# Turning x for the projections: TensorE transposes replaced by a copy within DRAM and VectorE block transposes, in a two-layer graph network whose order is written out by a planner

## The chip, the cores and the metric

The kernel runs on one core of a Trainium2 chip. The core has five engines that run their own instruction streams side by side: TensorE (PE in the profile; its weight loads are shown apart as PEld), VectorE (DVE), ScalarE (ACT), GpSimd (POOL) and SyncE (SP), which here only issues transfers. Each engine executes its instructions strictly in the order in which the program lists them, and an instruction that waits for a semaphore holds up everything behind it on that engine. Transfers run on 16 DMA engines. The metric is the time of one execution on the device in microseconds (us), and lower is better.

## The reference, cut to what matters

There are 16 graphs (batches) of 1024 nodes with 256 features, and a 0/1 adjacency matrix of 1024 x 1024 for each. Layer 0 is attention with 8 heads of 32 features, masked by the adjacency, then two layer norms and a matrix product; layer 1 is two graph attentions and a feed-forward network.

```python
# layer 0, per graph
q, k, v = heads(x @ Wq), heads(x @ Wk), heads(x @ Wv)
e = q @ k.T;  e = where(e >= 0, e, 0.2 * e)
h = softmax(where(adj > 0, e, NEG), axis=-1) @ v
x1 = layernorm(concat([layernorm(h), x]) @ Wffn.T) + x
# layer 1, per graph
h = gat(gat(x1, adj, W1, a1), adj, W2, a2)       # scores from two vectors, softmax over axis 1
r = layernorm(x1 + h)
out = layernorm(r + relu(r @ w_ff1 + b_ff1) @ w_ff2 + b_ff2)
```

All of it is float32. The products over features need x with its features on the partitions, that is, transposed: xT holds feature c*128 + p on partition p, for c = 0 and 1, and the nodes along the free axis. The change is in how xT is made from x, which lies in DRAM with a node per row.

## The kernel before, in words

The work is cut into 16 batches, one per graph. Within a batch the kernel makes xT in four pairs of node tiles (256 nodes each, `x_pair`), projects q and k (`qk_part`) and v (`v_part`), writes q and k to DRAM as a high and a low half and loads them back stacked for each head (`load_stacks`: the tiles qs and ks), and then goes through 8 heads of 8 key tiles: scores on PE (L615), leaky ReLU on ACT and DVE (L631, L633), the exponential on ACT (L636), the mask by a multiplication on POOL (L640), and the product with v on PE (L655). What follows the heads of a batch is `rest`: the norms, two graph attentions (L877 and L880 on DVE, L915 and L940 on PE) and the feed-forward network (L980 and L1008). The rest of one batch runs beside the heads of the next, and the projections for the batch after are made in the same time, so that in the middle of the run all three are in flight.

The order in which each engine gets its instructions is not written by hand. While the program is being built, a planner (`Order`) simulates the engines with costs given in the code. Every piece of work is a Python generator which yields what it needs next: `on(DVE=365)` for an engine and its planned cost in ns, `take` and `give` for buffers, `wait` and `fire` for events, `pause`, and `load` for transfers on SP (planned as 500 ns of SP each and 3500 ns of latency, or later where the planner's clock for all transfers says so). Among the pieces that could start within 300 ns of the earliest, the planner takes the one with the smallest aim, an absolute due time. The aims come from two tables in units of a slot, which is the planned time of one batch: `AIM` for most of the run and `EARLY` for what belongs to the first two batches. The planner's clock only fixes the order; on the chip, semaphores decide when an instruction runs.

The parts that the change and the steps of the prediction touch are these. `x_pair` (L461) takes a 2 KB buffer of the pool "pair" (18 of them, shared with the adjacency tiles, the q and k halves and others), issues one load of 256 nodes from ACT's queue (L466; 2 KB per partition), takes one of three PSUM banks ("misc"), transposes four 128 x 128 blocks on PE (L372 in `transposes`), copies the bank to xT by DVE or ACT, whichever the planner finds free first (L328 or L330 in `copy`), and fires the event that `qk_part` and `v_part` wait for. The node of row 2p+i of the pair goes to column i*128 + p. xT has two buffers, so that the pairs of the next batch can be made while the present one still uses its own. SP's queue carries the weights, the first batch's adjacency (L424), the halves of q and k (L504), the stacks (L581), x1 stored and fetched (L754, L761) and the output (L1023); ACT's queue carries x (L466) and the adjacency of the other batches (L420).

## Time and profile before

The kernel before takes 4320.45 us, the median of 3 runs (4317.54 to 4321.28). The profile is of one execution.

| what | value |
|---|---|
| time of the profiled execution | 4317.81 us |
| its span, from first to last instruction | 4315.9 us |
| PE busy | 4189.7 us (97%) |
| DVE busy | 3544.8 us (82%) |
| ACT busy | 2942.7 us (68%) |
| POOL busy | 2571.6 us (60%) |
| DMA engines busy, mean of 16 | some 28% |
| mean granted TensorE clock | 0.990 |

Busy time is the time in which an engine had at least one instruction under way. The end of a matmul is modelled, and matmuls overlap each other, so a PE that is busy is not PE at its peak; and the mean duration in a row of PE is that of one instruction from its start to its end, several of which are under way at once. A group of instructions is shown as line, engine, operation, tiles and shapes, then the count, busy time and mean duration, and after the bar the idle time of the engine ahead of them with what ended it.

### The profile page before, as it was taken

Reading aid. Unit: us, or ns where it says so; the run is one execution under the profiler, and the core shown is the slowest. Engines: PE = TensorE matmul, PEld = TensorE weight load, DVE = VectorE, ACT = ScalarE, POOL = GpSimd, SP = SyncE. Lnnn points to the kernel's source line nnn. Section 1 sums busy time; section 2 is a strip of 40 time slices with the busy share of each in tenths; the row PEclk is TensorE's granted clock in tenths of the full one; section 3 lists DMA queues with packets and bytes.
Section 4 is the critical chain, followed back from the end, with each engine's and each line's share of the span. In section 5 each row is a group of like instructions: output and inputs, shape, how many; then the busy total and the mean of one; then the engine's idle time right before and its main releaser. Section 6 shows DMA issues by size and latency. Waiting matters only on the chain.

```text
span 4315.9 us, 76274 instructions
## 1 busy us (share of the span) xinstructions
PE 4189.7 (97%) x30027; PEld 3030.3 (70%) x30027; DVE 3544.8 (82%) x5491; ACT 2942.7 (68%) x4362; POOL 2571.6 (60%) x1161
## 2 busy tenths in 40 slices
PE   8788999999999999999999999999999999999999
PEld 4466677677777777777777777777777777777687
DVE  6878878888888887879879788887889879788853
ACT  6756677777767677776776767677776776767632
POOL 5846467664757656574664757646575674747700
PEclk9999999999999999999999999999999999999999
DMA  6413223322232322323232222322323222222100
GB/s 188 125 54 99 69 76 87 91 72 86 74 94 67 96 84 68 90 71 89 84 84 81 79 81 79 91 73 81 91 74 89 81 84 84 74 79 57 30 20 21
DMA packets 156282, 344.79 MB, mean 80 GB/s; under 512 B 21750, under 2 KB 24332, under 8 KB 155916
## 3 DMA queue, kind: packets, MB, share of 16 engines
q1 hardware_dynamic: 112140, 260.13, 21.0%
q10 hardware_dynamic: 43776, 79.71, 6.6%
q8 instruction: 239, 3.92, 0.4%
q14 instruction: 127, 1.04, 0.1%
HBM read 239.09 MB, written 100.66 MB: 79 GB/s over the span
## 4 chain that ended last, share of the span: by engine, by line
PE 82%; DVE 11%; ACT 3%; POOL 1%; DMA 1%; issue 1%; SPq 0%; ACTq 0%; POOLq 0%; DVEq 0%
PE ps_a L655 17%; PE ps_s L615 11%; PE ps_m L915 10%; PE ps_m L980 9%; PE ps_m L940 9%; PE ps_m L1008 7%; PE ps_m L492 4%; DVE p L633 3%; PE ps_m L792 3%; PE ps_m L824 3%; PE ps_m L795 3%; PE ps_m L524 2%; PE ps_m L372 2%; DVE p L699 2%; POOL p L640 1%; DVE att L880 1%
## 5 line engine op out<-in xcount | busy, mean ns | idle before, releaser
L640 POOL TENSOR_TENSOR p<-p,mask 128x1024 f32<-128x1024 f32 x1024 | 2471.1, 2431 | 1425.5 <-ACT p L636 1044.1
L633 DVE TENSOR_TENSOR p<-p,ps_s 128x1024 f32<-128x1024 f32 x1024 | 1211.3, 1213 | 251.2 <-ACT p L631 248.1
L636 ACT ACTIVATE p<-p 128x1024 f32<-128x1024 f32 x1024 | 1082.2, 1059 | 302.3 <-DVE p L633 276.7
L631 ACT ACTIVATE p<-ps_s 128x1024 f32<-128x1024 f32 x1006 | 986.3, 1021 | 345.2 <-PE ps_s L615 283.0
L615 PE MATMUL ps_s<-qs,ks 128*128 128x512 f32 x2048 | 658.7, 437 | 30.6 <-DVE p L633 27.0
L655 PE MATMUL ps_a<-p,v 128*32 128x256 f32 x8192 | 561.9, 388 | 24.4 <-POOL p L640 24.3
L615 PEld LDWEIGHTS ps_s<-qs,ks 128*128 128x128 f32 x2048 | 352.6, 190 | 266.1 <-issue 114.8
L940 PE MATMUL ps_m<-y,att 128*128 128x256 f32 x2048 | 481.1, 382 | 12.6 <-ACT y L885 11.1
L915 PE MATMUL ps_m<-y,att 128*128 128x258 f32 x2048 | 477.1, 383 | 14.4 <-ACT y L885 12.9
L980 PE MATMUL ps_m<-rT,wf 128*128 128x256 f32 x2048 | 474.3, 383 | 9.4 <-ACT hid L989 4.3
L1008 PE MATMUL ps_m<-wf,hid 128*128 128x256 f32 x2048 | 475.7, 381 | 0.6 <-DVE hid L986 0.6
L915 PEld LDWEIGHTS ps_m<-y,att 128*128 128x128 f32 x2048 | 385.5, 190 | 89.3 <-ACT y L885 13.8
L980 PEld LDWEIGHTS ps_m<-rT,wf 128*128 128x128 f32 x2048 | 381.0, 190 | 85.9 <-issue 14.3
L699 DVE TENSOR_TENSOR p<-p 128x1024 f32<-128x1024 f32 x256 | 410.5, 1604 | 23.6 <-PE ps_a L655 23.4
L940 PEld LDWEIGHTS ps_m<-y,att 128*128 128x128 f32 x2048 | 378.4, 190 | 71.1 <-ACT y L885 11.3
L1008 PEld LDWEIGHTS ps_m<-wf,hid 128*128 128x128 f32 x2048 | 379.1, 190 | 63.6 <-issue 8.2
L655 PEld LDWEIGHTS ps_a<-p,v 128*32 128x32 f32 x8192 | 209.5, 109 | 289.3 <-issue 130.8
L655 PE MATMUL ps_a<-p,minus_ones 128*32 128x256 f32 x6144 | 405.8, 382 | 1.2 <-DVE p L699 1.2
L877 DVE SCALAR_TENSOR_TENSOR att<-first,second 128x1024 f32<-128x1024 f32 x256 | 359.7, 1405 | 32.4 <-ACT first L864 28.3
L880 DVE SCALAR_TENSOR_TENSOR att<-mask,att 128x1024 f32<-128x1024 fp8e4 x256 | 339.5, 1326 | 5.6
L655 PEld LDWEIGHTS ps_a<-p,minus_ones 128*32 128x32 f32 x6144 | 199.1, 111 | 138.3 <-issue 7.9
L885 ACT ACTIVATE y<-y,check 128x258 f32<-128x258 f32 x256 | 131.1, 512 | 220.4 <-DVE check L883 217.9
(101 smaller groups left out, 4330.0 us busy)
## 6 DMA issues: line engine op xcount, KB each, us to landing
qs<-qk_halves SPq DMA_DIRECT2D x256, 256.0 KB, 4.0
ks<-qk_halves SPq DMA_DIRECT2D x256, 256.0 KB, 5.2
adj_i<-in_adj_dram ACTq DMA_DIRECT2D x240, 256.0 KB, 3.1
qk_halves<-high SPq DMA_DIRECT2D x128, 256.0 KB, 2.8
qk_halves<-low SPq DMA_DIRECT2D x128, 256.0 KB, 3.6
xr<-in_x_dram ACTq DMA_DIRECT2D x64, 256.0 KB, 4.7
x_kept<-x SPq DMA_DIRECT2D x64, 256.0 KB, 2.0
x<-x_kept SPq DMA_DIRECT2D x64, 256.0 KB, 5.1
```

The costliest lines, as they stand in the source:

```text
L615: nc.tensor.matmul(ps[:, cols], kk[:, t * P:(t + 1) * P], q[:, cols], start=True, stop=True)
L631: nc.scalar.activation(p, ps, AF.Copy, scale=ALPHA)
L633: nc.vector.tensor_tensor(p, p, ps, op=OP.max)
L636: nc.scalar.activation(p, p, AF.Exp)
L640: nc.gpsimd.tensor_tensor(p, p, mask_of(b, t), op=OP.mult)
L655: nc.tensor.matmul(acc[i * DH:(i + 1) * DH, at:at + QN].rearrange("d (t r) -> d t r", r=DH), w, p.rearrange("k (t i r) -> k i t r", i=4, r ...
L699: nc.vector.tensor_tensor(ps[to], ps[to], ps[by], op=OP.add)
L880: nc.vector.scalar_tensor_tensor(e, mask_of(b, j), -1.0, e, op0=OP.mult, op1=OP.mult, accum_out=sums[:, j:j + 1])
L915: nc.tensor.matmul(pa[:, cols:cols + width], big[:, j, i * P:(i + 1) * P], rows[:, j, :width], start=(j == 0), stop=(j == NT - 1))
L940: nc.tensor.matmul(pa[:, i * D:(i + 1) * D], big[:, j, t * P:(t + 1) * P], y2[:, j, :D], start=(j == 0), stop=False)
L980: nc.tensor.matmul(pa[:, i * 2 * P:(i + 1) * 2 * P], wf1[:, dc, hc * P:(hc + 1) * P], rT[:, dc, :], start=(dc == 0), stop=(dc == DC - 1))
L1008: nc.tensor.matmul(pa[:, i * D:(i + 1) * D], hid[hc // 2][:, hc % 2, i * P:(i + 1) * P], wf2[:, hc, :], start=(hc == 0), stop=False)
```

## The change

x is first copied within DRAM, on SP's queue, so that the 256 features of each node are regrouped: for each of four ranges c, the features c*32 to c*32+31 of both halves (e = 0, 1) of the feature axis are laid side by side for all 256 nodes of the pair. That takes four transfers whose source is in runs of 32 floats (128 bytes). Four more transfers, also on SP's queue, load the result so that range c lies on the partitions 32c to 32c+31; each partition receives 512 bytes in each transfer, from two consecutive nodes. Two block transposes on DVE (`nc.vector.transpose`, which turns each block of 32 x 32 by itself) then write xT directly, one for each half of the features. The load on ACT's queue, the four transposes on PE, the PSUM bank and the copy out of it are gone. The two tables of aims and the length of a slot (253,000 to 251,000 ns) are replaced; names and formulas that use them are the same.

```diff
-    SLOT = 253e3
+    SLOT = 251e3
...
-    AIM = dict(mask0=0.602, x=1.454, x_step=-0.0104, mask=0.9396, mask_step=-0.0101, qk0=0.4907, qk1=1.7441,
...
-               ff_step=0.0063, fast0=0.2312, fast1=0.6979, fast15=1.0127, lead=14.8372)
...
+    AIM = dict(mask0=0.6069, x=0.5014, x_step=0.0732, mask=0.8735, mask_step=-0.1284, qk0=0.5927, qk1=2.165,
...
+               ff_step=-0.3151, fast0=0.0511, fast1=0.8537, fast15=0.9217, lead=25.7163)
...
-    EARLY = dict(x=2.6481, x_step=-0.1001, mask=0.5019, mask_step=0.0795, qk0=0.7532, qk1=1.2626, qk_step=-0.1325,
...
+    EARLY = dict(x=1.6699, x_step=-0.2106, mask=0.2894, mask_step=0.0581, qk0=1.041, qk1=1.0113, qk_step=-0.0303,
...
     def x_pair(b, u):
+        kept = dram.tile([4, 2 * P, DC, DH], FT, name=f"x_blocks{u}")
+        yield pause(1500)
+        yield load(2)
+        for c in range(4):
+            nc.sync.dma_start(kept[c], x[b, u * 2 * P:(u + 1) * 2 * P, :].rearrange("n (e c d) -> c n e d", e=DC, c=4)[c])
         yield take("pair")
-        xr = buf([P, 2, D], "pair", "xr")
-        yield pause(1500)
-        yield on(ACT=400, delay=3500)
-        nc.scalar.dma_start(xr, x[b, u * 2 * P:(u + 1) * 2 * P, :].rearrange("(p i) d -> p i d", p=P))
-        yield take("misc")
-        pt = misc()
-        yield on(PE=460)
-        transposes(pt, [xr[:, i, :] for i in range(2)])
+        xr = buf([P, 2 * D], "pair", "xr")
+        yield load(2)
+        for n in range(4):
+            nc.sync.dma_start(xr[:, n * P:(n + 1) * P],
+                              bass.AP(tensor=kept.tensor, offset=kept[0, n * 2 * DH].offset,
+                                      ap=[[2 * P * DC * DH, 4], [2 * DC * DH, DH], [1, 2 * DC * DH]]))
+        for dc in range(DC):
+            yield on(DVE=365)
+            nc.vector.transpose(xTs[b][:, dc, u * 2 * P:(u + 1) * 2 * P].rearrange("p (i n d) -> p i n d", i=2, n=4),
+                                xr.rearrange("p (n i e d) -> p e i n d", n=4, i=2, e=DC)[:, dc])
         yield give("pair")
-        engine = yield evacuate(2 * D)
-        copy(engine, xTs[b][:, :, u * 2 * P:(u + 1) * 2 * P], pt.rearrange("p (c n) -> p c n", c=DC))
-        yield give("misc")
         yield fire(("xT", b, u))
```

More of the change, by code (lines that the diff above doesn't have):

```diff
@@ L262, in unshifted_path @@
     NSCORE = 4 * NT
-    SLOT = 253e3
+    SLOT = 251e3
     PACE = SLOT / (H * NT // 2)
-    AIM = dict(mask0=0.602, x=1.454, x_step=-0.0104, mask=0.9396, mask_step=-0.0101, qk0=0.4907, qk1=1.7441,
-               qk_step=-0.0518, v0=0.7416, v1=0.621, v_step=0.0547, rows=-0.079, rows_step=-0.0113, first0=0.2137,
-               first1=-0.446, graph0=-0.0793, graph1=0.316, graph_step=0.0481, second=0.7493, second_step=-0.015,
-               normed=1.0223, normed_step=-0.0115, ff_wait=(None, 0, 1, 0), ff=(0.5532, 0.1074, 3.6996, 1.0353),
-               ff_step=0.0063, fast0=0.2312, fast1=0.6979, fast15=1.0127, lead=14.8372)
-    EARLY = dict(x=2.6481, x_step=-0.1001, mask=0.5019, mask_step=0.0795, qk0=0.7532, qk1=1.2626, qk_step=-0.1325,
-                 v0=0.2134, v1=1.5023, v_step=-0.0416, rows=-2.7213, rows_step=-0.3343, first0=-0.8482,
-                 first1=-4.695, graph0=0.0441, graph1=-0.9035, graph_step=-0.1073, second=0.463,
-                 second_step=0.0554, normed=0.7744, normed_step=0.0342, ff_wait=(None, 0, 1, 0),
-                 ff=(2.0875, 0.7055, 1.5112, 0.6358), ff_step=0.0607)
+    AIM = dict(mask0=0.6069, x=0.5014, x_step=0.0732, mask=0.8735, mask_step=-0.1284, qk0=0.5927, qk1=2.165,
+               qk_step=-0.0201, v0=0.7481, v1=0.3208, v_step=0.1901, rows=0.0369, rows_step=0.0451, first0=-1.6237,
+               first1=0.3549, graph0=-0.5452, graph1=0.5509, graph_step=-0.4716, second=0.7103, second_step=-0.043,
+               normed=1.0355, normed_step=0.0022, ff_wait=(None, 0, 1, 0), ff=(2.6641, -0.0482, 4.1277, 1.4124),
+               ff_step=-0.3151, fast0=0.0511, fast1=0.8537, fast15=0.9217, lead=25.7163)
+    EARLY = dict(x=1.6699, x_step=-0.2106, mask=0.2894, mask_step=0.0581, qk0=1.041, qk1=1.0113, qk_step=-0.0303,
+                 v0=0.5853, v1=0.9318, v_step=-0.11, rows=-2.7436, rows_step=-0.2322, first0=-0.0893,
+                 first1=-4.9016, graph0=0.1818, graph1=-1.3322, graph_step=-0.0812, second=0.7922,
+                 second_step=-0.0, normed=0.9294, normed_step=0.0301, ff_wait=(None, 0, 1, 0),
+                 ff=(2.1003, 1.4009, 2.1922, 1.2486), ff_step=0.0096)
     const = ctx.enter_context(tc.tile_pool(name="const", bufs=1))
```

## The prediction

> **What bounds the kernel now.** I read the page's shares of busy time first, then the same engines stage by stage, then who PE waits for.
>
> ```profile
> PE 4189.7 (97%) x30027; PEld 3030.3 (70%) x30027; DVE 3544.8 (82%) x5491; ACT 2942.7 (68%) x4362; POOL 2571.6 (60%) x1161
> ```
>
> ```profile
> 0.00:39.10 39.10, 30.04 (x142) 19.45 (x143) 11.85 (x25) 15.54 (x35) 0.83 (x9) 1.00 0.81 253
> 39.10:200.00 160.90, 128.31 (x1074) 61.15 (x1075) 141.54 (x135) 118.79 (x136) 148.63 (x68) 0.90 0.47 129
> 200.00:600.00 400.00, 359.40 (x2613) 255.45 (x2614) 311.45 (x486) 262.73 (x380) 229.05 (x108) 0.95 0.28 79
> 600.00:3900.00 3300.00, 3273.44 (x23775) 2378.01 (x23773) 2811.88 (x4368) 2340.07 (x3455) 2047.09 (x915) 1.00 0.29 82
> 3900.00:4315.90 415.90, 398.55 (x2430) 316.26 (x2426) 268.12 (x480) 205.53 (x358) 145.98 (x64) 0.98 0.10 29
> ```
>
> In the second fence each row is a stretch, its length, then the busy time of PE, PEld, DVE, ACT and POOL, the granted clock, the DMA share and GB/s. From 600 to 3900 us PE is idle for 3300.0 - 3273.4 = 26.6 us, under 1%: there the time is PE's work. Before 39 us it is a chain of transfers and projections with the DMA engines 81% busy. From 39 to 200 us POOL sets the pace (148.6 of 160.9 us). In the first 600 us PE is idle for 9 + 33 + 41 = 82 us, most of all its idle time. Who PE waits for between 600 and 3900 us:
>
> ```profile
> PE ps_a L655 <- POOL p L640: 6.6, 11, 0.6
> PE ps_s L615 <- DVE p L633: 5.5, 12, 1.1
> ```
>
> These are the two largest, in us, times and longest. DVE, though busy for 85% of that stretch, costs PE 5.5 us.
>
> **PE's part of the change.** The transposes that go, their copies, and the transfer that goes:
>
> ```profile
> L372 PE MATMUL ps_m<-ident,xr 128*128 128x128 f32 x256 | 36.7, 285 | 5.1 <-DMA xr<-in_x_dram 4.5 <-ACT hid L989 0.5
> L330 ACT COPY xT<-ps_m 128x512 f32<-128x512 f32 x49 | 27.4, 597 | 3.6 <-PE ps_m L372 3.6
> L328 DVE COPY xT<-ps_m 128x512 f32<-128x512 f32 x15 | 10.3, 688 | 2.2 <-PE ps_m L372 0.9
> ...
> xr<-in_x_dram ACTq DMA_DIRECT2D x64, 256.0 KB, 4.7
> ```
>
> What counts is how long they hold PE's stream, which the timeline shows around one place with three pairs in a row:
>
> ```profile
> 1305.38 1.47 PE L372 MATMUL ps_m<-ident,xr 128*128 128x128 f32 x12
> 1306.77 1.99 PE L1008 MATMUL ps_m<-wf,hid 128*128 128x256 f32 x8
> ```
>
> From the first start to that of the next work are 1.39 us for three pairs, 0.46 each; a lone pair at 781.64 is followed after 0.44. I take 0.45. Batch 0's four pairs are in the start, counted below, so 60 pairs x 0.45 = **27 us** less on PE. A rule of the Trainium skill ("TensorE: Matmul & The Clock Gate", Part 4: PE-mode transpose) gives some 275 ns for one transpose within a kernel. The row agrees for one instruction (median 273, mean 285), but four at 275 would be 1.1 us a pair and 66 us in all; the timeline shows them overlapped to a start every 0.11 us, so the rule's figure is a latency and I keep 27. The bounds are 26 (0.435) and 34 us (the row's busy time, 36.7/64 = 0.57).
>
> **ACT and DVE.** ACT loses 49 copies x 0.597 = 29 us and 64 issues x 0.335 (the median of an xr issue) = 21 us. It isn't the bound, so this is worth 0. DVE loses 15 x 0.688 = 10 us and gains 128 block transposes of 128x256. The nearest row is the block transpose of 128x512:
>
> ```profile
> L716 DVE STREAM_TRANSPOSE ho<-ps_a 128x512 f32<-128x512 f32 x128 | 91.5, 715 | 50.3 <-PE ps_a L655 48.3 <-DMA qk_halves<-high 0.2
> ```
>
> Half of it is 0.36 us; if a fixed part is kept (DVE copies from PSUM take 690 ns for 512 and 420 for 256) it is 715 - 270 = 0.445. I take 0.4: 128 x 0.4 = 51, net **+41 us** on DVE, 38 of them in batches 1 to 15. Its cover between 600 and 3900 us is 3300 - 2812 = 488 us of DVE idle, so I cost it at 0; without that cover it would be 38. The misc bank is no longer taken, and the pair buffer only from the reload on, which can only loosen other work.
>
> **The transfers.** Per pair SP issues eight transfers in place of ACT's one. An issue takes 0.335 us for 128 pieces (xr) and 0.468 for 256 (the four vectors a1, a2 at 154 us), so 4 x 0.47 + 4 x 0.4 = 3.5 us per pair, 224 us of SP in all. SP mostly waits (1237.8 us for the scores to free the stacks), and a head's stacks are asked for about a head, 32 us, ahead. The copies make 2048 pieces of 128 bytes per pair. Nothing in the trace copies within DRAM. From below: in the us from 157 to 158 the engines took some 940 pieces under 512 bytes with 150 of 1 KB and were full, which leaves about 8 ns for a tiny piece, so 2048 x 8 / 16 = 1.0 us. From above: one 2 KB piece of the xr queue took 104 ns (6.6% of 16 x 4316 us over 43776 packets); 2048 x 104 / 16 = 13 us. I take 15 ns, near the tiny pieces since the bytes are few: 1.9 us a pair, plus 2.0 us to land as the stores to DRAM (x_kept) take, behind 1.9 us of issuing: about 6 us.
>
> The reload's nearest row:
>
> ```profile
> x<-x_kept SPq DMA_DIRECT2D x64, 256.0 KB, 5.1
> ```
>
> So the data is there some 1.6 + 5 = 6.6 us after SP starts to issue it. Here a rule speaks against the change: "DMA: Bandwidth & Descriptors", under why a DMA increments its semaphore by 16, says that a transfer is spread over the largest number up to 16 that divides the slowest dimension of both its sides. The reload's source has 4 there, so 4 engines, not 16. By an estimate from the 1 KB pieces and the tiny ones, a 512-byte piece takes about 30 ns: 512 of them are 1.0 us over 16 engines and 3.8 over 4. No transfer of this trace shows such a case, so I keep both: 6.6 or about 9 us.
>
> The planner allows 1.0 us of SP and at least 3.5 to land, up to 6.1 us in all by its own transfer clock. DVE is in order, so a block transpose placed there waits 0.5 to 3 us for its data, with the next leaky ReLU (L633) behind it, then ACT's exponential and POOL's mask, and PE at last. But DVE already waits up to 3.0 us for ACT's copy of the scores, 188 times between 600 and 3900 us, 186 us in all, and PE feels 5.5 of it. A low aim also puts the transposes behind other DVE work. I pass on **+2 us**; bounds 0 and 60 (1 us a pair).
>
> **The start.** Four pairs' copies and reloads now stand in front of the first projection, and what was in ACT's queue is in SP's, ahead of the adjacency loads and, behind them, the first stacks.
>
> ```profile
> 0.75 1.87 ACTq L466 DMA_DIRECT2D xr<-in_x_dram  x4
> 2.27 7.07 SPq L424 DMA_DIRECT2D adj_i<-in_adj_dram  x8
> 14.16 3.60 PE L492 MATMUL ps_m<-xT,wk 128*128 128x512 f32 x8
> 39.12 1.68 PE L615 MATMUL ps_s<-qs,ks 128*128 128x512 f32 x4 [1.88 <-DMA ks<-qk_halves]
> ```
>
> After the weights at 2.2 us, 16 issues of copies end at about 10 us; some adjacency loads get in between; the reloads are issued from 11 to 21 and the last lands at about 26, where the q and k projections of the second node half could start. Today projections start at 14.2 us, so from above this is **+12 us**. From below it is 0: the chain from there to the scores (25 us) runs through transfers that compete with adjacency loads (landing up to 9 us), of which more will be done. I take +6. POOL paces what follows up to 200 us, so the delay goes through.
>
> **The new aims** reorder all engines. The trace can't price an order that it hasn't run. Below: a third of the 82 idle us of the first 600, so -27. Above: PE 1% less busy from 600 us on, +33. I take 0.
>
> **Sum.** -27 + 0 + 0 + 2 + 6 + 0 = -19, so a span of 4315.9 - 19 = 4297, a profiled execution of 4299 (1.9 us lie around the span), and since that execution was 2.6 us under the runs' median, **4301 us**. A run of this kernel can be told from no change at about 0.2%, 8.6 us: 4312 and 4329 are the marks.
>
> **Rivals.**
> - *The order helps as well* (4274): the new aims close a third of the early idle time beside the 19 us. For it: PE's clock is 0.90 and 0.95 in those stretches, so it has room; against: POOL's 149 us there stay.
> - *The gain is spent* (4320): the start costs 12 and the order 7 us more in the steady stretch. For it: PE at 99% leaves little to win from order. Against: that same 99% says that work taken from PE shows.
> - *DVE waits for the reloads* (slower; 4341): 0.7 us a pair reaches PE, 60 x 0.7 = 42 where I took 2. It turns the sign at 19/60 + 2/60 = 0.35 us a pair, and is slower by the mark at 0.5. For it: the planner's 4.5 to 6.1 us against my 6.6 to 9. Against: PE's 5.5 us above, and the p buffers (six) between DVE and PE.
>
> **How the numbers follow.** Chances: forecast 0.50, the order helps 0.20, the gain is spent 0.09, DVE waits 0.21. The first two are faster by over 0.2% except for the forecast's upper edge (0.02, the same), the third counts as the same except 0.03 (slower), the fourth is slower except 0.01 (the same): faster 0.68, same 0.09, slower 0.23. The forecast's own range is 4288 to 4314. To leave out no more than 2 in 10 the range takes in the helping order down to 4270 and DVE's wait up to 4343.
>
> **What would show it.** PE's busy time down by 27 us, and its share from 600 us on still 98 to 99%; no row of L372 with xr; 128 block transposes of some 0.4 us; the first scores (L615) at 42 to 51 us in place of 39; the waits of DVE for xr under 1 us each, with PE's waits for L633 unchanged. I am wrong if DVE's waits for xr come to over 40 us with PE's share below 98%, if the first scores come after 55 us, or if a slot of the steady stretch (260 us now) is not 1 to 2.5 us shorter.

## The result, and the profile after

The changed kernel takes 4369.00 us (median of 4 runs, 4364.34 to 4369.17) beside 4318.99 us for the kernel before (median of 4 runs, 4313.07 to 4321.28). The ratio is 1.0115, with a 95% interval of 1.0098 to 1.0133: slower by about 50 us, where 19 us less was forecast. The profiled execution of the changed kernel took 4369.12 us with a span of 4367.3 us, so the two spans differ by 51.4 us, and these are what the traces have to explain. In the changed file the lines behind `x_pair` stand four further down (L615 became L619, L980 became L984, L989 became L993).

The page's shares of busy time, and the stretches (start:end, length, busy PE, PEld, DVE, ACT and POOL, granted clock, DMA share, GB/s), after:

```profile
PE 4166.3 (95%) x29771; PEld 3017.4 (69%) x29771; DVE 3609.7 (83%) x5595; ACT 2926.1 (67%) x4322; POOL 2546.0 (58%) x1161
```

```profile
0.00:39.10 39.10, 17.13 (x89) 13.58 (x90) 8.54 (x21) 7.81 (x18) 0.83 (x9) 1.00 0.67 190
39.10:200.00 160.90, 124.48 (x906) 57.80 (x904) 128.43 (x128) 103.28 (x119) 119.76 (x55) 0.86 0.53 144
200.00:600.00 400.00, 354.60 (x2581) 239.98 (x2578) 332.22 (x511) 268.34 (x391) 244.06 (x112) 0.94 0.31 85
600.00:3900.00 3300.00, 3228.35 (x23456) 2357.41 (x23454) 2825.16 (x4356) 2314.05 (x3383) 2019.94 (x915) 1.00 0.31 85
3900.00:4367.00 467.00, 441.74 (x2747) 348.63 (x2746) 315.34 (x582) 232.60 (x414) 161.37 (x72) 0.99 0.11 33
```

PE did lose work: 4189.7 to 4166.3 us, 23.4 less. But it stands idle 75 us more, and 75 - 23 is the difference. From 600 to 3900 us its idle time went from 26.6 to 71.7 us (3300.0 - 3228.35), which is 5.7 us of a slot in place of 2.1; before 39 us it went from 9 to 22, and at the tail from 17 to 25. The first scores of each batch, as the timeline has them, divide the 51.4 us in another way (a slot is the time from one batch's first scores to the next one's):

| part | before | after | difference |
|---|---|---|---|
| first scores of the first batch | 39.1 | 57.0 | +17.9 |
| from there to those of the second | 168.9 | 179.6 | +10.7 |
| the next four slots | 1029.2 | 1032.0 | +2.8 |
| the ten slots after them, each | 260.17 | 261.5 | +1.3, +13.1 in all |
| from the last batch's first scores to the end | 477.0 | 483.8 | +6.9 |

Who PE waits for from 600 to 3900 us after the change (us in all, times, longest):

```profile
PE ps_m L984 <- ACT hid L993: 30.5, 25, 1.7
PE ps_a L659 <- DVE p L703: 8.5, 10, 0.9
...
PE ps_s L619 <- DVE p L637: 3.0, 5, 1.5
```

The first two waits were hardly there before. The second's counterpart (L655 for L699) is not in the list of that stretch, and the first's is this line:

```profile
PE ps_m L980 <- ACT hid L989: 2.1, 2, 1.2
```

The wait for hid is now larger than PE's whole idle time was. None of these lines names x. The transfers are not what the engines wait for in the steady stretch: over PE, its weight loads, DVE, ACT and POOL the waits for any transfer come to 7.6 us there (21.2 before), none of them for x, and DVE waits for xr 7.1 us in 4 times, all at the start. The block transposes are as costed, the duration being min/median/max in ns:

```profile
L476 DVE STREAM_TRANSPOSE xT<-xr x128: 395/404/447, 22.4 to 3746.8; 128x256 f32<-128x256 f32 x128
```

The start in the changed kernel, from the timeline (start, duration, engine, line; SPq is SP's queue, where the duration is that of the issuing):

```profile
2.26 10.62 SPq L466 DMA_DIRECT2D x_blocks<-in_x_dram  x16
12.92 2.04 SPq L424 DMA_DIRECT2D adj_i<-in_adj_dram  x4
15.00 2.60 SPq L471 DMA_DIRECT2D xr<-x_blocks  x4
...
20.55 9.52 SPq L471 DMA_DIRECT2D xr<-x_blocks  x12
...
31.90 1.88 PE L496 MATMUL ps_m<-xT,wk 128*128 128x512 f32 x4
...
57.03 2.05 PE L619 MATMUL ps_s<-qs,ks 128*128 128x512 f32 x4 [3.58 <-DMA ks<-qk_halves]
```

The sixteen copies are issued at 0.66 us each and the reloads at 0.65 to 0.79. The first projections of q and k come at 31.9 us where they came at 14.2, and the first scores at 57.0 where they came at 39.1.

### The profile page after: what moved, and what is told of

It reads as the page before. It is cut to its first block, busy times and chain, and to the rows that moved or that the text cites. A ratio compares the mean times of both kernels' runs of the same rounds, so it can differ in the third digit from the quotient of the medians.

```text
span 4367.3 us, 76417 instructions
## 1 busy us (share of the span) xinstructions
PE 4166.3 (95%) x29771; PEld 3017.4 (69%) x29771; DVE 3609.7 (83%) x5595; ACT 2926.1 (67%) x4322; POOL 2546.0 (58%) x1161
## 3 DMA queue, kind: packets, MB, share of 16 engines
q14 instruction: 132, 1.08, 0.1%
## 4 chain that ended last, share of the span: by engine, by line
PE 65%; DVE 20%; ACT 7%; issue 2%; POOL 1%; DMA 0%; ACTq 0%; DVEq 0%
PE ps_a L659 13%; PE ps_m L919 10%; PE ps_s L619 8%; PE ps_m L1012 7%; PE ps_m L944 7%; PE ps_m L984 7%; DVE p L637 6%; PE ps_m L496 4%; DVE att L884 3%; DVE att L881 3%; ACT p L635 2%; PE ps_m L796 2%; PE ps_m L799 2%; PE ps_m L828 2%; PE ps_m L528 2%
## 5 line engine op out<-in xcount | busy, mean ns | idle before, releaser
L637 DVE TENSOR_TENSOR p<-p,ps_s 128x1024 f32<-128x1024 f32 x1024 | 1215.2, 1213 | 283.0 <-ACT p L635 279.6
L619 PE MATMUL ps_s<-qs,ks 128*128 128x512 f32 x2048 | 641.1, 432 | 40.7 <-DVE p L637 27.9
L619 PEld LDWEIGHTS ps_s<-qs,ks 128*128 128x128 f32 x2048 | 356.4, 191 | 236.3 <-issue 110.0
L984 PE MATMUL ps_m<-rT,wf 128*128 128x256 f32 x2048 | 468.1, 381 | 33.8 <-ACT hid L993 32.2
L703 DVE TENSOR_TENSOR p<-p 128x1024 f32<-128x1024 f32 x256 | 468.3, 1829 | 21.7 <-PE ps_a L659 21.2
L984 PEld LDWEIGHTS ps_m<-rT,wf 128*128 128x128 f32 x2048 | 381.4, 190 | 108.3 <-ACT hid L993 46.2
L884 DVE SCALAR_TENSOR_TENSOR att<-mask,att 128x1024 f32<-128x1024 fp8e4 x256 | 364.7, 1424 | 7.4
L881 DVE SCALAR_TENSOR_TENSOR att<-first,second 128x1024 f32<-128x1024 f32 x256 | 342.6, 1338 | 11.2 <-ACT first L868 9.0
```

Of the source, the lines that this page charges most:

```text
L619: nc.tensor.matmul(ps[:, cols], kk[:, t * P:(t + 1) * P], q[:, cols], start=True, stop=True)
L637: nc.vector.tensor_tensor(p, p, ps, op=OP.max)
L881: nc.vector.scalar_tensor_tensor(e, first[:, 0, :], second[:, j:j + 1], first[:, 1, :], op0=OP.mult, op1=OP.max)
L884: nc.vector.scalar_tensor_tensor(e, mask_of(b, j), -1.0, e, op0=OP.mult, op1=OP.mult, accum_out=sums[:, j:j + 1])
L984: nc.tensor.matmul(pa[:, i * 2 * P:(i + 1) * 2 * P], wf1[:, dc, hc * P:(hc + 1) * P], rT[:, dc, :], start=(dc == 0), stop=(dc == DC - 1))
```

## The experiments

The theory drawn from these lines: the saving on PE is real, and three things eat it, namely the start, the order from the new tables, and the fact that PE's time was not worth its face value. The rivals: DVE waits for the reloads or is slowed by the block transposes, and PE with it; or the transfers disturb what SP issues besides.

### The start: the first batch's x made the old way in the new order

```diff
     def x_pair(b, u):
+        if b == 0:
+            yield pause(1500)
+            yield load(2)
+            yield take("pair")
+            xr = buf([P, 2, D], "pair", "xr")
+            yield load(2)
+            nc.scalar.dma_start(xr, x[b, u * 2 * P:(u + 1) * 2 * P, :].rearrange("(p i) d -> p i d", p=P))
+            ps = psum.tile([P, N], FT, tag="scores", name="ps_x")
+            yield on(DVE=365)
+            transposes(ps, [xr[:, i, :] for i in range(2)])
+            yield on(DVE=365)
+            nc.vector.tensor_copy(xTs[b][:, :, u * 2 * P:(u + 1) * 2 * P],
+                                  ps[:, :2 * D].rearrange("p (c n) -> p c n", c=DC))
+            yield give("pair")
+            yield fire(("xT", b, u))
+            return
```

> The changed kernel with its order as it is, but the first batch's x loaded as in the kernel before (from ACT's queue, where the reload stands), transposed by PE into a scores bank and copied by DVE where the block transposes stand. If the copies and reloads at the start are what makes the first scores 18 us late, they come at 40 to 45 us and the time is 4369 - 15 = 4354 us; if the late start is the new order's or is absorbed by the first batch, which POOL paces, 4365 to 4369 us. Either way the steady slots stay at 261.5 us.

It took 4346.92 us, a ratio of 1.0071 (1.0054 to 1.0087): 22 us less than the changed kernel, and by the two ratios 19. The first scores come at 47.4 us in place of 57.0; the rest is won right after them (the first x1 is stored at 249.8 us in place of 266.4). The slot stays at 261.5 us, and the largest waits of the steady stretch are the same to a tenth (L984's for hid, L1000 in this file, 30.5 us in 25 times). So making the first batch's x in the new way costs about 20 us. The start is not back where it was, though:

```profile
22.04 1.88 PE L512 MATMUL ps_m<-xT,wk 128*128 128x512 f32 x4
47.37 2.05 PE L635 MATMUL ps_s<-qs,ks 128*128 128x512 f32 x4 [3.33 <-DMA ks<-qk_halves]
```

The first projections of q and k, at 14.2 us before, come at 22.0, and the first scores 8.3 us later than before, with x of that batch made as it was: so much of the changed kernel's late start goes with the new order. The profiled spans of this kernel and the one before differ by 29.8 us: 8.3 to the first scores, 4.1 in the first slot, -1.8 in the next four, 13.2 in the ten after them and 5.9 at the end.

### The tables: the new ones with the old x, and one number of each

The new tables and slot length with x made the old way; then each kernel with the other's slot length alone.

```diff
-    SLOT = 253e3
+    SLOT = 251e3
...
-    AIM = dict(mask0=0.602, x=1.454, x_step=-0.0104, mask=0.9396, mask_step=-0.0101, qk0=0.4907, qk1=1.7441,
+    AIM = dict(mask0=0.6069, x=0.5014, x_step=0.0732, mask=0.8735, mask_step=-0.1284, qk0=0.5927, qk1=2.165,
...
-    EARLY = dict(x=2.6481, x_step=-0.1001, mask=0.5019, mask_step=0.0795, qk0=0.7532, qk1=1.2626, qk_step=-0.1325,
+    EARLY = dict(x=1.6699, x_step=-0.2106, mask=0.2894, mask_step=0.0581, qk0=1.041, qk1=1.0113, qk_step=-0.0303,
```

> The kernel before with the new tables and slot length, x made in the old way. Theory 'order': the order that the new tables give is worse by itself, and with PE's transposes back it is worse than the changed kernel apart from its start: more than 4319, about 4369 + 26 - 18 = 4377 us or above. Rival 'mechanism': the tables are as good as the old ones, 4310 to 4325 us.

4425.50 us, ratio 1.0255 (1.0238 to 1.0272), with slots that run from 252 to 279 us.

```diff
-    SLOT = 253e3
+    SLOT = 251e3
```

> The kernel before with one number changed: the slot length 251,000 instead of 253,000 ns, which scales all aims; x in the old way. Theory 'order' (the order is a fragile product of tables and costs, and swings by more than the 27 us that the change takes from PE): slower by over 50 us. Rival (small changes of the tables move little, so that the loss must lie in the new way of making x): within 10 us of 4319.

4416.79 us, ratio 1.0238 (1.0222 to 1.0254): this one number costs the kernel before 103 us.

```diff
-    SLOT = 251e3
+    SLOT = 253e3
```

> The changed kernel with the slot length of before, 253,000 ns; nothing else. Theory 'order': slower than 4369 by over 30 us, since its tables fit its own costs and slot as the old ones do theirs. Rival: within 10 us of 4369.

4449.42 us, ratio 1.0310 (1.0294 to 1.0325): the opposite edit costs the changed kernel 80 us.

In all three PE is idle for 97 to 118 us between 600 and 3900 us. What follows is less than I had hoped for: the new tables with the old x are not "the order's part" of the change, since the planner makes another order from them once x costs something else. An order is fitted to one set of costs and aims: moving the unit of all aims by 0.8% moved the time by 80 to 103 us. The parts must therefore be taken apart with the order held.

### The new x in the old order

With the old tables and the planner told the old costs, every other instruction keeps its place, and the new transfers and block transposes stand where the old load and PE transposes stood.

```diff
-        xr = buf([P, 2, D], "pair", "xr")
+        xr = buf([P, 2 * D], "pair", "xr")
+        kept = dram.tile([4, 2 * P, DC, DH], FT, name=f"x_blocks{u}")
+        for c in range(4):
+            nc.sync.dma_start(kept[c], x[b, u * 2 * P:(u + 1) * 2 * P, :].rearrange("n (e c d) -> c n e d", e=DC, c=4)[c])
         yield pause(1500)
         yield on(ACT=400, delay=3500)
-        nc.scalar.dma_start(xr, x[b, u * 2 * P:(u + 1) * 2 * P, :].rearrange("(p i) d -> p i d", p=P))
+        for n in range(4):
+            nc.sync.dma_start(xr[:, n * P:(n + 1) * P], ...)
         yield take("misc")
-        pt = misc()
         yield on(PE=460)
-        transposes(pt, [xr[:, i, :] for i in range(2)])
+        for dc in range(DC):
+            nc.vector.transpose(xTs[b][:, dc, ...], xr[...])
         yield give("pair")
-        engine = yield evacuate(2 * D)
-        copy(engine, xTs[b][:, :, u * 2 * P:(u + 1) * 2 * P], pt.rearrange("p (c n) -> p c n", c=DC))
+        yield evacuate(2 * D)
         yield give("misc")
```

> The kernel before with its own tables and so its own order on every engine, but x made in the new way: the copies within DRAM are put on SP's queue where the planner hands out the pair buffer, the reloads where the load stood, the two block transposes on DVE where PE's transposes stood; nothing else moves. Theory 'order' (the new way itself saves PE time, the loss comes from the order that the new tables give): a steady slot of 260.2 - 1.75 = 258.4 us, but the first scores some 10 to 18 us late as in the changed kernel, so about 4319 - 26 + 15 = 4308 us. Rival 'mechanism' (copies, SP's queue or block transposes hold up DVE and PE in every batch): a slot of 261.5 us or more as in the changed kernel, 4350 us or more.

4445.84 us, ratio 1.0302 (1.0285 to 1.0319), first scores at 54.1 us. The same with the first batch's x left as it was:

```diff
+    def x_pair(b, u):
+        yield from (x_pair_new if b else x_pair_old)(b, u)
```

> As the run before it, but the first batch's x is made in the old way. Theory 'order': the start is that of the kernel before (first scores at 39 us) and each of the later slots is 1.75 us shorter: 4319 - 26 = 4293 us, 15 us under the run before it. Rival 'mechanism': 4335 us or more, with the first scores at 39 us all the same.

4428.23 us, ratio 1.0262 (1.0245 to 1.0279), slots of about 267.3 us. The start is worth 18 us here too. The rest is the rival: DVE's wait for the reloads, which here is real. The waits of DVE from 600 to 3900 us, and 5 us of the stretches:

```profile
DVE xT L492 <- DMA xr<-x_blocks: 52.5, 21, 7.8
```

```profile
2155.00:2160.00 5.00, 4.90 (x13) 3.64 (x14) 5.00 (x4) 1.53 (x2) 3.70 (x2) 0.69 0.50 119
```

The second line comes right after three waits of PE of 2.23, 2.57 and 1.73 us within 10 us: PE is busy for 4.90 of 5 us, at a granted clock of 0.69. Eight matmuls of L1033 took 1.89 us at 2143.98 us, ahead of the waits, and 2.86 at 2156.13, behind them. So the waits here cost more than their length.

Asking earlier did not help. Here the copies are issued when the piece of work begins, and the reloads when its buffer is there, ahead of the old load's place:

```diff
+        kept = dram.tile([4, 2 * P, DC, DH], FT, name=f"x_blocks{u}")
+        for c in range(4):
+            nc.sync.dma_start(kept[c], ...)
         yield take("pair")
-        xr = buf([P, 2, D], "pair", "xr")
+        xr = buf([P, 2 * D], "pair", "xr")
+        for n in range(4):
+            nc.sync.dma_start(xr[:, n * P:(n + 1) * P], ...)
         yield pause(1500)
```

> As f2_old_order_new_x_but_first (old tables and order, first batch in the old way), but the transfers of x stand earlier on SP: the copies where the batch's projections begin, the reloads where the pair buffer is handed out; the block transposes stay where PE's transposes stood. If what cost 7 us a slot there was the block transposes meeting reloads that were still under way, DVE's waits for xr go and the slot becomes 260.2 - 1.75 = 258.4 us, in all about 4293 us. If the new way costs by itself (block transposes on DVE, SP's issues, traffic), the slot stays above 260.2 us and the time above 4330 us.

4531.44 us, ratio 1.0504 (1.0490 to 1.0518):

```profile
DVE xT L492 <- DMA xr<-x_blocks: 140.0, 12, 24.2
```

In this order a batch's x cannot begin before an xT buffer is free, so the four pairs are asked for in one place, and copies and reloads take turns on SP's queue at 7.5 to 7.8 us a pair. DVE then waits for the last, once a slot. The copies were then issued a whole batch ahead:

```diff
     def x_pair_new(b, u):
+        if b == 1:
+            x_blocks(b, u)
         yield take("pair")
...
+        if b + 1 < B:
+            x_blocks(b + 1, u)
         yield give("pair")
```

> As f2_old_order_new_x_but_first (old tables and order, first batch in the old way, reloads where the load stood, block transposes where PE's transposes stood), but from the third batch on the copies within DRAM are issued one batch ahead, right after the same pair's block transposes of the batch before, so that the reloads neither queue behind them nor wait for them. If late data was the whole loss of f2, DVE's waits for xr (52.5 us between 600 and 3900 us there) fall under 10 us and the slot is 258.4 us, in all about 4295 us. If block transposes on DVE, SP's issues or the traffic cost by themselves, the slot stays above 260.2 us with no waits for xr to show for it, and the time is above 4330 us.

4346.72 us, ratio 1.0081 (1.0067 to 1.0095). The waits for xr are gone, and PE is busy for 256.8 us of a slot, where it was 258.1 (its share of the stretch from 600 to 3900 us, times the slot). Still the slot is 261.1 us in most cases, longer than the 260.17 before. PE now waits for the leaky ReLU (L649 for L667, 23.5 us where it was 5.5). And the slots are not all of the loss: the first one takes 180.0 us where it took 168.9. There the rival about SP's queue is real. The copies for the second batch stand in it ahead of an adjacency load of the first, which is issued at 43.24 us where it was at 30.51, and this is DVE's wait for it, which PE shares for 10.7 us:

```profile
DVE adj_b L429 <- DMA adj_i<-in_adj_dram: 11.7, 1, 11.7
```

In the changed kernel DVE's longest wait for an adjacency load behind the first scores is 0.9 us. The suspect in the slots was DVE's further work, so the block transposes were replaced by plain copies of the same shape on ACT, which leave the values unturned:

```diff
         for dc in range(DC):
-            nc.vector.transpose(xTs[b][:, dc, ...], xr[...])
+            nc.scalar.copy(xTs[b][:, dc, ...], xr[...])
```

> As f5_old_order_copy_batch_ahead, but the two block transposes of each pair are replaced by two plain copies of the same shape on ACT, at the same place, so that from the second batch on xT holds rows of x that are not transposed within their blocks: the part left out is the turning itself, and DVE is relieved of it, while PE and all transfers do what they did. If the block transposes on DVE, where PE's transposes stood, are what still holds PE up in f5 (PE's idle time 4.3 us a slot there against 2.1 before), the idle time goes back to about 2 us and the slot to 258.4 to 259 us, in all 4310 to 4320 us with f5's late first batch (180 us against 169). If the lighter PE simply runs into the next wait of that order, or the transfers do it, the slot stays at 260.5 to 261.1 us and the time at 4340 us or more.

4338.47 us, ratio 1.0054 (1.0040 to 1.0068). The wait for the leaky ReLU goes back to 6.0 us, and others stand in its place: the projections for DVE's low half (13.6 us), for ACT's copies of xT (9.0), L1014 for ACT's z (7.4). The slot is 261.0 us. So one wait takes another's place, and a slot with less PE work is no shorter either way, though here ACT carries the copies, and the wait for them is one of the new ones. Then DVE was relieved in another place, by giving all evacuations of the hidden layer to ACT, in the kernel with the copies a batch ahead and in the kernel before:

```diff
             engine = yield on(DVE=395, ACT=370)
+            engine = "ACT"
```

> As f5_old_order_copy_batch_ahead, but every evacuation of a hidden part (hid) that the planner gave to DVE is put on ACT at the same place in the order: some 8 a slot of 0.48 us, 4 us a slot off DVE, four of them just ahead of the place of x's transposes. If DVE is what is short at that place, PE's wait for L633's counterpart there (1.7 us a slot) goes and the slot falls from 261.1 to about 259 us; if not, or if ACT becomes short instead, it stays at 261 us or grows.

4384.22 us, ratio 1.0161 (1.0148 to 1.0175).

> The kernel before with the same move of hid from DVE to ACT and nothing else, to tell what that move is worth by itself. DVE costs PE 5.5 us between 600 and 3900 us there, so at most 0.4 us a slot can be won: 4310 to 4325 us.

4346.75 us, ratio 1.0072 (1.0059 to 1.0086). By the ratios the move costs 35 and 31 us, about alike (a miss: nothing of the kind was expected in the kernel before). Relieving DVE in this place helps neither kernel, and the pair tells nothing about the block transposes apart from that.

### What PE's time is worth

My sum rested on "work taken from PE shows". It can be tested without any new transfer: in the kernel before, only one of the four transposes of a pair is made from the second batch on, and the copy reads it four times (xT is then not the reference's).

```diff
-        transposes(pt, [xr[:, i, :] for i in range(2)])
+        nc.tensor.transpose(pt[:, :P], xr[:, 0, :P], ident)
...
-        copy(engine, xTs[b][:, :, u * 2 * P:(u + 1) * 2 * P], pt.rearrange("p (c n) -> p c n", c=DC))
+        copy(engine, xTs[b][:, :, u * 2 * P:(u + 1) * 2 * P].rearrange("p c (i n) -> p c i n", i=2),
+             pt[:, None, None, :P].to_broadcast([P, DC, 2, P]))
```

> The kernel before with its tables and order, but from the second batch on only the first of each pair's four transposes on PE is made, and the copy out of the bank reads that block four times (so x is transposed for one quarter and repeated in the other three: the left-out part is three of four transposes). Transfers, ACT, DVE and POOL are untouched. It asks what PE's time at that place is worth by itself: three quarters of 1.75 us, 1.3 us a slot, less on PE. Theory 'bound' (the prediction's: PE's work is the time): the slot falls from 260.2 to 258.9 us, 4318 - 18 = 4300 us. Theory 'shadow' (PE's transposes there stood beside a wait that comes anyway, for q and k's evacuations or for DVE): the slot stays within 0.4 us of 260.2 and PE's idle time grows by what was taken.

4316.18 us, ratio 1.0008 (1.0000 to 1.0016). PE has 1.05 us less work in a slot, and the slot is 260.15 us as before: that time was worth nothing. Where it went can be read. The chain of waits of the kernel before, around 2086 us (start, duration, what):

```profile
2086.26 1.31 PE ps_m L372 x12
2087.57 1.90 PE ps_m L1008 x8
...
2095.26 4.41 DMA qk_halves<-low
2099.68 0.59 ACT z L330
2100.32 0.70 PE ps_m L980 x2
```

Three of a batch's four pairs stand at 2086.26, while DVE evacuates the hidden layer and makes an xT; the fourth stands beside a store of a q or k half, whose landing frees a pair buffer, behind which ACT copies z, for which L980 waits. With the transposes taken out, PE arrives earlier and waits for exactly these. The timeline of PE in the kernel with one of four (in brackets the idle time before, and for what):

```profile
2084.60 1.99 PE L1028 MATMUL ps_m<-wf,hid 128*128 128x256 f32 x8 [0.66 <-DVE xT L328]
...
2091.12 1.98 PE L512 MATMUL ps_m<-xT,wq 128*128 128x512 f32 x4 [0.16 <-DVE low L517]
```

Over the stretch PE's wait of L1028 for xT is 7.6 us where it wasn't in the list before, and that for z is 6.2 in place of 2.6. PE at 99% looked like the limit; other chains of the slot were just as long at that spot. One reserve: the wait for xT is for a copy out of the bank, which stays in this kernel and is gone in the changed one, so 7.6 of the 16 us are not shown to be lost there too.

To see whether that holds for every place and both signs, three more in the old order. Four further transposes for each pair, ahead of the v projection's matmuls, which overwrite them:

```diff
         yield on(PE=895)
+        if b and g == 0:
+            for j in range(4):
+                nc.tensor.transpose(pa[:, j * P:(j + 1) * P], ident, ident)
```

> The kernel before with the same four further transposes for each pair from the second batch on, ahead of the v projection's matmuls, on top of those that it has. Theory that PE sets the steady stretch (99% busy): each shows in full, 27 us, a slot of 262.0 and some 4343 us. Theory of the shadow, as the kernel with one transpose of four left showed for less work: less shows, a slot of 260.2 to 261.2. A slot of 262.0 here beside 260.15 there would say that PE's place is just at the edge: less work on PE gains nothing, more work costs in full.

4339.54 us, ratio 1.0054 (1.0040 to 1.0068), slot 261.9.

```diff
-        transposes(pt, [xr[:, i, :] for i in range(2)])
+        for _ in range(2 if b else 1):
+            transposes(pt, [xr[:, i, :] for i in range(2)])
```

> The kernel before with the four transposes of each pair of x made twice from the second batch on, the second time into the same bank: the same 27 us as in the kernel with further transposes at the v projections (4339.54 us), but in the place where the change takes them away. Theory of the shadow with room left: less than 27 us, 4314 to 4330. Theory of the edge: in full, some 4340 us.

4327.35 us, ratio 1.0032 (1.0020 to 1.0045), slot 261.1. PE's wait for z, 2.6 us before, is no longer in its list.

```diff
+        dcs = 1 if b and g == 0 else DC
         for i in range(2):
-            for dc in range(DC):
+            for dc in range(dcs):
                 nc.tensor.matmul(pa[:, i * P:(i + 1) * P], ...
-                                 wv[:, dc, g * P:(g + 1) * P], start=(dc == 0), stop=(dc == DC - 1))
+                                 wv[:, dc, g * P:(g + 1) * P], start=(dc == 0), stop=(dc == dcs - 1))
```

> The kernel before, and from the second batch on the v projection of the first group of heads takes one of the two halves of the features: half of its matmuls are left out, so v is not the reference's there. A v projection of a pair holds PE for 133.3 us / 128 = 1.04 us, so 0.52 us less for each of 60 pairs, 31 us in all, taken from PE in another place than the transposes of x. Theory of the edge (another chain is as long as PE's work, so that less work on PE gains nothing anywhere): slot 260.15, no change. Theory of the place (only where the transposes of x stood was there something else to wait for): slot 258.1, some 4284 us.

4301.65 us, ratio 0.9973 (0.9964 to 0.9982), slot 259.1: 12 of the 31 us. A wait that is new in PE's list takes a part of the rest:

```profile
PE ps_m L861 <- ACT v L534: 6.6, 12, 0.6
```

And in the new order, the first batch's x being made the old way, first with the four transposes given back to PE at the v projections (the same edit as above), then with half of those projections left out:

> The new order with the first batch's x made the old way (4346.92 us, slot 261.5), and PE given back the work that the change took from it: from the second batch on, four transposes of 128x128 for each pair of x, written to the bank of the v projection just before its matmuls, which overwrite them; nothing else reads them. Theory that PE's time counts in the new order: 60 x 0.45 us = 27 us, a slot of 263.3 and some 4374 us. Theory that the work stood and stands in the shadow of other engines (the waits for hid, p and z): part of it goes into waits that shrink, a slot of 261.5 to 262.4 and 4347 to 4360 us.

4373.57 us, ratio 1.0129 (1.0114 to 1.0145), slot 262.8.

> The new order with the first batch's x made the old way (4346.92 us, slot 261.5), and the same half of the v projections left out. If PE's time counts in the new order in both directions: 31 us less, some 4316 us, a slot of 259.5 or up to 1.4 us less where part of it shows at the ends. If added work costs there (the kernel with the transposes given back to PE) but work taken away gains nothing: 4347 us.

4342.98 us, ratio 1.0069 (1.0055 to 1.0083), slot 260.9. Together, for the whole run. PE's work is the difference of its busy time in a slot (its share of the stretch from 600 to 3900 us, times the slot) over 15 slots; the time is against the kernel that each was made from:

| order | where | PE's work, us | time, us |
|---|---|---|---|
| old | transposes of x, three of four left out | -16 | none, or up to 7 more |
| old | transposes of x, made twice | +17 | +14 |
| old | v projections, four transposes more | +24 | +25 |
| old | v projections, half of one group's left out | -25 | -12 |
| new | v projections, four transposes more | +26 | +27 (25 by the ratios) |
| new | v projections, half of one group's left out | -21 | -4 (1 by the ratios) |

Neither of the two theories was right alone. Work added to PE costs over 80% of its length, and work taken away gains between nothing and half of it, in both orders. That is what an order looks like in which several chains are about equally long: lengthening PE's shows, and shortening it runs into the next.

### The steady stretch of the new order: without block transposes

The kernel of the first experiment, with plain copies on ACT in the place of the block transposes (the values are left unturned):

```diff
             yield on(DVE=365)
-            nc.vector.transpose(xTs[b][:, dc, ...], xr[...])
+            nc.scalar.copy(xTs[b][:, dc, ...], xr[...])
```

> As f4_new_order_first_old (the changed kernel's order, the first batch's x in the old way), but from the second batch on the two block transposes of each pair are plain copies of the same shape on ACT, at the same place: the turning within blocks is left out. DVE is relieved of 3.1 us a slot, ACT gets about 3 us more. If DVE's added work is what keeps PE idle for 5.7 us a slot in the new order, the slot falls from 261.5 to 259 us or below; if the idle time is the order's own (PE meeting the hidden parts' evacuations on ACT), it stays at 261 us or grows with ACT's load.

4354.08 us, ratio 1.0096 (1.0080 to 1.0111), slot 261.5. PE's largest wait is what it was:

```profile
PE ps_m L1000 <- ACT hid L1009: 30.4, 25, 1.7
```

ACT's copies of xT, which are new here, cost PE 0.5 us. So neither the block transposes nor DVE's further work makes these waits. The same 30 us of them stand in the kernel with the first batch's x made the old way and in the one with the four transposes given back: they go with the order. Of the 25 waits 15 are of 0.93 us, where L984 waits for ACT to evacuate L984's own earlier results. The other ten, once a slot, are of 1.65, and one of them can be read from the chain of waits of the changed kernel:

```profile
2401.04 3.06 DVE att L884 x2
...
2404.20 1.21 DVE p L637
...
2405.44 0.04 ACT p L640
...
2406.40 0.46 ACT hid L993
...
2406.91 3.72 PE ps_m L984 x16
```

L984 waits 1.65 us for ACT's hid, which stands in ACT's queue behind an exponential, which waits for DVE's leaky ReLU, which stands behind a graph attention operation that took 3.04 us in place of its median of 1.22. All ten of these waits come 5.9 us after the start of such an operation, of 3.04 or 3.05 us. PE's second wait is of the same kind. It also comes once a slot, ten times 0.85 us, each time behind a join (L703, the sum of two tiles of p on DVE) of 3.13 to 3.15 us:

```profile
2358.63 3.13 DVE L703 TENSOR_TENSOR p<-p 128x1024 f32<-128x1024 f32 x1
2361.82 1.50 PE L659 MATMUL ps_a<-p,minus_ones 128*32 128x256 f32 x24 [0.85 <-DVE p L703]
```

Together these two are 25 of the 45 us by which PE's idle time grew between 600 and 3900 us. Why the DVE instructions were long is in the last section.

## Why the prediction was wrong

**PE's part, -27: the size was right, its worth was not.** PE is busy for 23.4 us less. But I took "PE is idle for under 1%, there the time is PE's work" as the price of that time in both directions, and in the old order 16 us of this work, taken out with the copies left in, gained nothing. What I had in hand and didn't use: the chain of waits of the kernel before runs through SP, a store of a q or k half and ACT's z right beside these transposes. In the new order as much work, given back at the v projections, cost 25 to 27. So the term has no value of its own; it depends on the order and the place that it is taken from.

**The start, +6 with a bound of +12: measured some 20.** Two parts of the working were too small. SP issues a copy within DRAM every 0.66 us and a reload every 0.65 to 0.79 at the start, where I had taken 0.47 from a transfer of half as many pieces and 0.40 from one of as many, but larger ones, so the last reload is issued at 30.1 us, not at 21. And the forecast of a compensation, fewer adjacency loads beside the later chain, didn't come. Of the delay of 17.7 us at the projections of q and k, 9.9 go when the first batch's x is made the old way; at the scores it is 9.7 of 17.9, and the rest of the 20 us is lost behind them. The other 8 us of the late start go with the new order, the next term.

**The new aims, 0 with bounds of -27 and +33: this is the step that failed most.** It was put at nothing because the trace could not price it, not because anything spoke for nothing. With as much PE work as before and the first batch's x made the old way, the new order is at a ratio of 1.0129, 56 us longer; without that work it is at 1.0071, 31 us; with the start at 1.0115, 50 us. Those are the three terms, +56, -25 and +19, where I had 0, -27 and +6. The first of them still holds the transfers and the block transposes of the later batches beside the order. The experiment without block transposes speaks against those, and that no engine waits for x, and all of them together for no more than 7.6 us of transfers in the steady stretch, speaks against the transfers; but no kernel made all of x the old way in this order, so that the whole of it is the order's is argued. Shown are the waits that the order brings in the steady stretch, 25 us of them behind DVE instructions which it puts under POOL's. My bound of 1% of PE was a guess at how far an order can move things; one number of the tables moves either kernel by 80 to 103 us.

**DVE's and ACT's work, 0: right for the block transposes.** They take 404 ns as against 0.4 us, and in the new order the kernel with ACT's copies in their place is not faster. But DVE's busy time grew by 65 us, not by 41: the joins alone take 58 us more, in the order that I had put at 0. **DVE's waits for the reloads, +2: right in the changed kernel**, where they are 7.1 us, all at the start, and none in the steady stretch for which the term was meant. As a rival it had the right sign for the wrong reason, so that its 4341 lay nearer than the others is luck. It is what happens where the order doesn't leave room: 52 and 140 us of waits in the old order with the new x. **The transfers: right.** A piece of 128 bytes takes 13 ns (the median of the 131,072 in the trace), where I took 15; the first pair's reload was there 7.3 us after SP began to issue it, between my 6.6 and 9. I had left open whether a reload is spread over 16 engines or 4, and the trace says 4. Its 512-byte pieces, 27 ns each, are never more than 8 under way at once, as two transfers over 4 engines each would have it. The queue also has 5120 more pieces of 4 bytes than before. ACT's queue has 16 of these for each of its loads (4864 for 304 before the change), and 16 for each of the 256 copies leave 4 for each of the 256 reloads. The first pair's pieces took 3.5 us from first to last, beside my estimate of 3.8 for 4 engines.

What I had named as signs of being wrong came out so: the first scores after 55 us, and a slot that isn't shorter. The rival "the gain is spent" was the nearest in its mechanism, with a costlier start and a slower steady stretch, and was still 49 us short. (Its 4320 comes out only if its 12 us at the start stand on top of the forecast's 6; with 12 in all it is 4314.) No kernel tried here that computes the whole reference is faster than the one before.

## What to carry to other kernels

In both orders of this kernel, an engine busy for 98 to 99% of a stretch was a bound for work that was added, not for work that was taken away. Before a saving on it is counted, look in the chain of waits for what else runs at that very spot, and if it can be had, run the old order with nothing but that work left out. Where an order is fitted to its costs, a change of costs together with new tables is a new order, and its term needs a bound as wide as a small change of the tables makes (here 80 to 103 us), not zero. In a new order, look at which DVE instructions with two inputs in SBUF start under an instruction of POOL. Transfers at the head of a run are priced by the number of issues times the duration of one, with the duration taken from an issue of the same kind; the number of pieces alone misled here.

## What the hardware showed that I had not expected

How long the issue of a transfer takes is not told by its number of pieces alone: 0.335 us for 128 of 2 KB (on ACT's queue), 0.468 for 256, and a median of 0.62 us for the copies of 512 pieces within DRAM, but 0.64 us for the reloads, which have 128 pieces of 512 bytes.

Several short waits of PE were followed by a lower clock, though none was longer than 2.6 us: three of 2.23, 2.57 and 1.73 us within 10 us, and then 5 us at 0.69, in the kernel with the new x in the old order.

DVE instructions with both inputs in SBUF wait for POOL. The graph attention operation (L880 before, L884 after), 1.22 us at its median, takes up to 3.05 us in some places: 14 of 200 lasted over 1.8 us between 600 and 3900 us before the change, 26 of 200 after. The joins (L699 before, L703 after) show it more often, as the page's means have it:

```profile
L699 DVE TENSOR_TENSOR p<-p 128x1024 f32<-128x1024 f32 x256 | 410.5, 1604 | 23.6 <-PE ps_a L655 23.4
L703 DVE TENSOR_TENSOR p<-p 128x1024 f32<-128x1024 f32 x256 | 468.3, 1829 | 21.7 <-PE ps_a L659 21.2
```

Of 203 joins in that stretch 75 lasted over 1.8 us before, 106 after. In all 40 attention operations and all 181 joins over 1.8 us POOL was in the middle of its mask multiplication when DVE began, and every one of them ended 1.08 or 1.09 us after POOL's instruction did. Those that began with no POOL instruction under way took 1.19 to 1.23 us. It works the other way too: seven times after the change the attention operation and the multiplication began within 1 ns of each other, DVE took 1.22 us and POOL 3.2, where its median is 2.24. The leaky ReLU (L637), with one input in PSUM and one in SBUF, is the counterexample: 551 of them began under POOL's multiplication after the change, and none took over 1.23 us. The operation at 2401.04 us stands under this one:

```profile
2400.68 2.32 POOL L644 TENSOR_TENSOR p<-p,mask 128x1024 f32<-128x1024 f32 x1 [0.76 <-ACT p L640]
```

POOL's ends at 2403.00 and DVE's at 2404.08, 1.08 us later. The Trainium skill ("SBUF — State Buffer", SBUF: two separate sides) has a rule that fits: DVE, when it reads two inputs from SBUF, and a GpSimd instruction that reads SBUF share a pair of ports as an exclusive lock, and whichever starts first keeps it for the whole instruction. By the median alone this operation would have ended 1.8 us earlier and the joins of 3.13 us 1.9 us earlier, more than the 1.65 and 0.85 us that PE then waits, so this may be the cause of both places' waits; no kernel was run with the two apart, and that part stays argued.
